# A graph network's gather: four tiles in every 320 loaded row by row from SyncE's queue

## The chip, the cores and the metric

One NeuronCore of a Trainium2 chip. The metric is the device time of one execution in microseconds, as the median of several runs. The kernel is written in Bass with the Tile framework, which puts the semaphores in and decides much of the order of instructions on each engine.

## The reference

Two layers of an equivariant graph network over the same graph: 6250 nodes with 160 features (64 scalars and 32 vectors of three components) and 200000 edges, sorted by destination. Each layer transforms the nodes, gathers the transformed row of every edge's source, multiplies it with weights that a small network makes from the edge's embedding and with the edge's attributes, sums over the edges of each destination, transforms the sums, and normalises. Of layer 0, cut to what matters here:

```python
x1s, x1v = ...                       # transformed nodes, 160 numbers a node
weight = silu(edge_length_embedded @ W_fc1) @ W_fc2
gs = x1s[edge_src]                   # the gather: one row of 640 bytes per edge
gv = x1v[edge_src]
mid0a = w0 * gs * e_s
...
agg = segment_sum(edge_feat, edge_dst, num_segments=n) / sqrt(16.0)
...
x = layernorm(x + layer0(x, ...))
x = layernorm(x + layer1(x, ...))
```

Layer 1 has the same form, with an embedding of 64 numbers per edge in place of 10 and 224 weights in place of 192. Everything is float32.

## The kernel before

**Tiles.** The edges are cut into 1563 tiles of 128 edges, one edge a partition (`NT`). Two tiles make a pair, two pairs a unit: 391 units. Each layer is one pass over the units in the function `windows(i, ...)`, i being 0 or 1. A prologue makes the first layer's table of transformed nodes, `table[0]`, in DRAM; pass 1 of the edges makes `table[1]` from its sums, and pass 2 gathers from that. (If the destinations don't fit the kernel's windows, another branch, `general`, computes everything; the inputs here don't take it.)

**The loop.** `windows` steps u from -4 to 391. In step u it issues
- `gather` for the pairs of unit u + 4: one indirect DMA per tile, issued by POOL (GpSimd), that fetches the 128 rows of `table[i]` named by the tile's sources into the tile `g` (L703). There are 8 buffers of `g`, one a pair;
- `weights` of unit u + 2 on PE (TensorE) and `hidden` of unit u + 3 on PE and ACT (ScalarE): the small network's two layers. `hidden` asks for the inputs `e`, a chunk of 8 tiles at a time, through SP's queue (SP is SyncE; `inputs`, L634 in pass 1, L642 in pass 2), into three tiles in turn (`inputs_of`). It asks for a chunk and the one after it;
- `places` and `products` of unit u + 2 on DVE (VectorE): the selection matrix from destinations and attributes (L734), and the products of gathered rows and weights, `mid` (L721);
- `aggregate` of unit u: matmuls on PE that sum the products by destination in PSUM; `turn` adds a finished group to the sums in SBUF (L778 loads the group's first destination into a register, L781 and L783 add);
- between these, `prepare` and `proceed` do the node work, one step at a time. `fetch` loads a block of nodes into the tile `nx` through SP (L486, L488, L545). In pass 1 `own_nodes` computes the self part of half of the blocks early, through a tile `ne` with one buffer, and stores it to DRAM (L471).

Sources (`src`) and attributes (`ea`) of 48 tiles are loaded at once through SP (`scalars`, L611 and L612), into two buffers each. The call stands where a tile of a new chunk is first needed:

```python
def of(t):
    if ("c", t // CH) not in made:
        scalars(t // CH)
```

**What sets the order.** On PE the order is the program's (`keep_in_program_order`, L138 and L143 are the helpers' lines, which all matmuls share). On the other engines and for the DMAs Tile's scheduler orders the instructions within what the data allow. SP's and ACT's DMAs go out in the order of their queues: an SP instruction that waits holds up all that stand behind it. Each of these DMAs uses one of eight completion semaphores in turn, and waits for the DMA that used it before.

Of the kernel before, what the change touches and what calls it, by code (L numbers as in the profile page):

```python
# [9 lines left out]
F32 = mybir.dt.float32  # L10
I32 = mybir.dt.int32
# [3 lines left out]
ET = mybir.EngineType  # L15

P = 128
N = 6250
E = 200000
S, V = 64, 32  # L20
D = S + 3 * V
NB = (N + P - 1) // P
NT = (E + P - 1) // P
# [3 lines left out]
CH = 48  # L27
EC = 8
BG = 4
ZERO = 8  # L30
ROWS = P * NB + P
EPS = 1e-5
C_S = math.sin(math.pi / 8.0)
# [53 lines left out]
def kernel(ctx: ExitStack, tc: tile.TileContext, a, out):  # L87
# [19 lines left out]
    nc = tc.nc  # L107
# [3 lines left out]
    work = prologue.enter_context(tc.tile_pool(name="first", bufs=2))  # L111
# [7 lines left out]
    table = [dram.tile([N, D], F32, name=f"table{i}") for i in range(2)]  # L119
# [30 lines left out]
    for bs in chunks:  # L150
        x = work.tile([P, BG, D], F32, name="xg", bufs=len(chunks))
# [67 lines left out]
    at = 0  # L219
# [244 lines left out]
    def own_nodes(b, work):  # L464

        n = rows_of(b)
        rows = slice(b * P, b * P + n)
        (fetch, self_part, self_mix), _ = second_nodes(b, work, False, "ne")

        def store():  # L470
            nc.scalar.dma_start(xown[rows, :], self_mix()[:n])  # L471
            owned.add(b)

        return [fetch, self_part, store]

    def second_nodes(b, work, clear, name="nx"):


        n = rows_of(b)
        rows = slice(b * P, b * P + n)  # L480
        st = {}

        def fetch():
            x = st["x"] = work.tile([P, D], F32, name=name, bufs=4 if name == "nx" else 1)
            if b in owned:
                nc.sync.dma_start(x[:n], xown[rows, :])  # L486
            else:
                nc.sync.dma_start(x[:n], a["x_main"][:, b, :] if b < NB - 1 else a["x_tail"])  # L488

        def self_part():  # L490
            st["xs"] = turned(st["x"][:n], work, "pn", 1)

        def self_mix():
            x = st["x"]
            q = mixed(st["xs"], n, wsc, "pn", 1)
            for k in range(2):
                nc.vector.scalar_tensor_tensor(x[:n], q[:, k, :], own[:n, b, k:k + 1], x[:n],
                                               op0=OP.mult, op1=OP.add)
            return x

        def summed():
            p = psum.tile([P, 512], F32, name="pn", bufs=1)
            q = p[:n, :2 * D].rearrange("p (w d) -> p w d", w=2)
            for c in range(4):
                l = sm[:96, c, rows]
                if c < 2:
                    matmul(q[:, :, 0:S + V], l, rm0[:, c], start=(c == 0), stop=False)
                else:
                    v = S + (c - 1) * V
                    matmul(q[:, :, 0:S], l, rm0[:, c, :, 0:S], start=False, stop=False)  # L510
                    matmul(q[:, :, v:v + V], l, rm0[:, c, :, S:], start=False, stop=False)
            matmul(q[:, :, S + V:D], sr[:64, rows], rr0, start=False, stop=True)
            y = st["x"][:n]
            for k in range(2):
                nc.vector.scalar_tensor_tensor(y, q[:, k, :], gets[:n, b, k:k + 1], y,
                                               op0=OP.mult, op1=OP.add)
            mv = work.tile([P, 8], F32, name="mv")
            normed(y, mv)

        def turn():  # L520
            st["xt"] = turned(st["x"][:n], work, "pn", 1)

        def mix():
            xt = st["xt"]
            p = psum.tile([P, 512], F32, name="pn", bufs=1)
            matmul(p[:n, 0:P], xt[:, 0, :n], who[0][:, :P], start=True, stop=True)
            matmul(p[:n, P:D], xt[:V, 1, :n], who[1][:, :V], start=True, stop=True)
            r = work.tile([P, D], F32, name="nr")
            nc.scalar.activation(r[:n], p[:n, 0:D], AF.Copy, scale=nv[:n, b, 0:1])
            nc.scalar.dma_start(table[1][rows, :], r[:n])  # L530
            nc.scalar.dma_start(xmid[rows, :], st["x"][:n])
            if clear:
                nc.vector.memset(sm[:, :, b * P:b * P + P], 0.0)
                nc.vector.memset(sr[:, b * P:b * P + P], 0.0)

        return [fetch] + [self_part, self_mix] * (b not in owned), [summed, turn, mix]
# [47 lines left out]
        return [fetch, self_part, self_mix], [summed]  # L584


    def windows(i, loads, work, inputs_of):
        nw = (192, 224)[i]


# [9 lines left out]
        made = {}  # L600
# [24 lines left out]
        def inputs(c):  # L625

            e0 = c * EC * P
            n = min(EC * P, E - e0)
            k, of_e = ((10, a["e10"]), (64, a["e64"]))[i]
            e = inputs_of[c % 3]  # L630

            for h in range(2):
                if i == 0 and n == EC * P:
                    nc.sync.dma_start(  # L634
                        e[h * 64:h * 64 + k].rearrange("p (u m) -> p u m", m=2 * P),
                        of_e[:, e0:e0 + n].rearrange("p (u h m) -> p u h m", h=2, m=2 * P)[:, :, h])
                    continue
                for u in range(0, n, 4 * P):
                    r = u + h * 2 * P
                    m = min(2 * P, n - r)  # L640
                    if m > 0:
                        nc.sync.dma_start(e[h * 64:h * 64 + k, u // 2:u // 2 + m],  # L642
                                          of_e[:, e0 + r:e0 + r + m])
            made["e", c] = e
# [34 lines left out]
        def weights(ps):  # L679
# [5 lines left out]
            for p, j in [(p, j) for p in ps for j in range(2)] if i == 0 else \  # L685
                    [(p, j) for j in range(2) for p in ps]:
                t = 2 * p + j
                if t < NT:
# [5 lines left out]
                        l, r = h[k, j * P:j * P + n], fc2[1][k]  # L694
                    matmul(made["w", p][:n, j, :nw], l, r, start=True, stop=True)

        def gather(p):
            g = work.tile([P, 2, D], F32, name="g", bufs=8)
            for j in range(2):
                t = 2 * p + j  # L700
                if t < NT:
                    n = edges_of(t)
                    nc.gpsimd.indirect_dma_start(  # L703
                        out=g[:n, j, :], out_offset=None, in_=table[i][:, :],
                        in_offset=bass.IndirectOffsetOnAxis(ap=of(t)[0], axis=0))
            made["g", p] = g
# [117 lines left out]
        for u in range(-4, units + 1):  # L824
# [7 lines left out]
                weights(pairs_of(u + 2))  # L832
            if 0 <= u + 3 < units:
                hidden(u + 3)
            if 0 <= u + 2 < units:
                for p in pairs_of(u + 2):
                    places(p)
                    products(p)
# [131 lines left out]
    with tc.If(ok > 0) as cmp:  # L970
        with tc.tile_pool(name="loads", bufs=2) as loads, \
                tc.tile_pool(name="edges", bufs=2) as work:

            inputs_of = [loads.tile([P, EC * P // 2], F32, name=f"e{k}", bufs=1) for k in range(3)]
            for e in inputs_of:
                nc.vector.memset(e, 0.0)
            for i in range(2):
                windows(i, loads, work, inputs_of)
    with cmp.Else():
        pinned[0] = False  # L980
        owned.clear()
# [54 lines left out]
```

## Time and profile before

| | |
|---|---|
| median of 3 runs | 4095.0 us (4084.81 to 4096.76) |
| the profiled execution | 4098.12 us, its span 4096.3 us |
| mean granted clock of TensorE | 0.900 |
| busy in the span | PE 3522.1 us (86%), DVE 3095.1 us (76%), POOL 3026.7 us (74%), ACT 1176.1 us (29%) |
| POOL's gathers, L703 | 3126, the first starts at 65.8 us, the last at 4056.9 us |
| pause of POOL between the passes | 34.6 us, for the last blocks of nodes |
| moved by DMA | 364.05 MB, 89 GB/s on average |

Busy time is an average over the span; an engine that is busy for less than all of it may still be the one that all others wait for, if each of its instructions is followed by a fixed pause. SP computes nothing: its instructions are DMA issues, waits and register steps, and the profile does not count them as busy. They are seen in the timeline and by line, where a duration is the time that the issue takes on SP's queue, not the transfer's.

The profile's lines name the kernel's lines; "out<-in" are tiles. For a group, the numbers are the busy time in us, the mean in ns, and the engine's idle time just before its instructions with what ended most of it.

### The profile page before, as it was taken

The page shows a single profiled execution, that of the slowest core. Times are in us where ns is not written, and L with a number is a line of the kernel's source. Part 1 is how long each engine was busy: PE and PEld are TensorE (multiplying, and loading weights), DVE is VectorE, ACT ScalarE, POOL GpSimd, SP SyncE. Part 2 cuts the span into 40 slices and gives each one's busy share as a digit, 9 for nine tenths or more (in the row PEclk, how much of TensorE's full clock was granted, in tenths as well). Part 3 has the DMA queues.
Part 4 walks back from the last instruction along what each step waited for, and adds up shares of the span by engine and source line. Part 5 has one row for each costly group of instructions (what it writes and reads, how often), then busy time and mean ns, then how long its engine had stood idle before and what let it go on. Part 6 is the DMA issues. An engine that isn't in the chain of part 4 may idle for free. (4 is left out here: it accounts for less than half of the span.)

```text
span 4096.3 us, 108196 instructions
## 1 busy us (share of the span) xinstructions
PE 3522.1 (86%) x37363; PEld 2419.1 (59%) x37363; DVE 3095.1 (76%) x13202; ACT 1176.1 (29%) x4013; POOL 3026.7 (74%) x3232
## 2 busy tenths in 40 slices
PE   7788988889899999999978888888788888888887
PEld 5565666666666666666655555555555555555555
DVE  6676666667777777777757777777778888888887
ACT  2122221222222333333311111122223333444454
POOL 4777777777777777777757777777777777777774
PEclk8899898889899999999978888889989999998998
DMA  4233322222222232333323333333333333333332
GB/s 128 78 84 87 81 75 77 78 76 79 77 79 79 79 82 79 82 84 80 87 71 94 96 95 97 98 96 96 100 97 97 103 100 96 106 100 98 101 103 59
DMA packets 298517, 364.05 MB, mean 89 GB/s; under 512 B 86323, under 2 KB 246204, under 8 KB 297964
## 3 DMA queue, kind: packets, MB, share of 16 engines
q0 software_dynamic: 151056, 257.36, 23.8%
q1 hardware_dynamic: 121740, 85.59, 7.4%
q10 hardware_dynamic: 25168, 14.11, 1.1%
q8 instruction: 300, 4.92, 0.5%
q14 instruction: 253, 2.07, 0.2%
HBM read 338.73 MB, written 18.03 MB: 87 GB/s over the span
## 5 line engine op out<-in xcount | busy, mean ns | idle before, releaser
L703 POOL DMA_INDIRECT g<-table,src x3126 | 3004.9, 961 | 1026.8 <-issue 736.9
L721 DVE TENSOR_TENSOR mid<-g,pw 128x128 f32<-128x128 f32 (+2 forms) x7820 | 1852.8, 299 | 653.0 <-DMA g<-table,src 416.1
L138 PE MATMUL pw<-fc,h 100*128 100x192 f32 (+1 forms) x6252 | 1225.5, 383 | 193.4 <-DVE mid L721 186.4
L138 PE MATMUL pg<-mid,sel 128*32 128x160 f32 (+1 forms) x25008 | 1155.1, 305 | 0.0
L138 PEld LDWEIGHTS pw<-fc,h 100*128 100x128 f32 (+1 forms) x6252 | 895.9, 203 | 369.9 <-issue 315.0
L138 PEld LDWEIGHTS pg<-mid,sel 128*32 128x32 f32 x25008 | 755.3, 116 | 387.7 <-issue 320.7
L734 DVE SCALAR_TENSOR_TENSOR sel<-iota,off,ea 128x128 f32<-128x128 f32 x3126 | 940.5, 341 | 39.4 <-PE pg L138 35.0
L138 PE MATMUL pair<-e,fc 64*100 64x256 f32 (+1 forms) x2348 | 606.2, 454 | 120.2 <-DVE sr L783 113.4
L665 ACT ACTIVATE h<-pair 100x256 f32<-100x256 f32 x782 | 260.7, 381 | 954.6 <-PE pair L138 941.0
L138 PEld LDWEIGHTS pair<-e,fc 64*100 64x100 f32 (+1 forms) x2348 | 239.5, 183 | 351.2 <-issue 193.1
L676 ACT ACTIVATE h<-pair 128x256 f32<-128x256 f32 x392 | 150.5, 384 | 960.5 <-PE pair L138 795.6
L143 PE MATMUL pair<-ident,r 128*96 128x128 f32 (+1 forms) x852 | 225.7, 291 | 27.6 <-ACT h L665 21.7
L138 PE MATMUL pn<-rm,sm 96*128 96x128 f32 (+4 forms) x980 | 192.1, 356 | 51.2 <-DVE sm L781 49.6
L759 ACT ACTIVATE r<-pg 128x96 f32<-128x96 f32 (+1 forms) x568 | 149.5, 263 | 297.8 <-PE pg L138 228.5
L781 DVE TENSOR_TENSOR sm<-pair,sm 96x128 f32 (+1 forms) x568 | 161.9, 285 | 92.1 <-PE pair L143 19.1
L143 PEld LDWEIGHTS pair<-ident,r 128*96 128x96 f32 (+1 forms) x852 | 107.8, 127 | 206.0 <-issue 105.3
L765 ACT ACTIVATE rest<-pg 32x32 f32<-32x32 f32 x1136 | 209.5, 184 | 12.5
L138 PEld LDWEIGHTS pn<-rm,sm 96*128 96x128 f32 (+3 forms) x980 | 176.3, 235 | 59.9 <-DVE sm L781 53.3
L138 PE MATMUL pn<-rr,sr 64*128 64x128 f32 (+2 forms) x196 | 66.1, 426 | 93.4 <-DVE sr L783 89.0
L458 ACT ACT_TABLE_LOAD x97 | 124.5, 1283 | 7.1 <-DVE mv L457 5.4
L138 PEld LDWEIGHTS pair<-fold,rest 128*128 128x128 f32 x568 | 104.0, 226 | 1.1 <-ACT rest L765 1.1
L783 DVE TENSOR_TENSOR sr<-pair,sr 64x32 f32 (+1 forms) x568 | 99.7, 176 | 0.8 <-DVE sm L781 0.6
(137 smaller groups left out, 1313.0 us busy)
## 6 DMA issues: line engine op xcount, KB each, us to landing
g<-table,src POOLq DMA_INDIRECT x3126
e<-in_e SPq DMA_DIRECT2D x781, 64.0 KB
e<-in_e SPq DMA_DIRECT2D x390, 20.0 KB
ea<-in_ea_main SPq DMA_DIRECT2D x63, 96.0 KB
xg<-in_x_main SPq DMA_DIRECT2D x12, 320.0 KB
table<-rg SPq DMA_DIRECT2D x12, 320.0 KB
xmid<-nx ACTq DMA_DIRECT2D x48, 80.0 KB
table<-nr ACTq DMA_DIRECT2D x48, 80.0 KB
```

Source lines behind the costliest of these rows:

```text
L138: r = nc.tensor.matmul(*args, **kw)
L143: r = nc.tensor.transpose(*args)
L458: nc.scalar.activation(mv[:n, 1:2], mv[:n, 1:2], AF.Sqrt, bias=eps[:n])
L665: nc.scalar.activation(h[:100, 2 * P * j:2 * P * j + m], pair[j][:100, :m], AF.Silu)
L676: nc.scalar.activation(h[:kk, c0:c1], p[:kk, c0:c1], AF.Silu, scale=0.125)
L703: nc.gpsimd.indirect_dma_start(out=g[:n, j, :], out_offset=None, in_=table[i][:, :], in_offset=bass.IndirectOffsetOnAxis(ap=of(t)[0], axis=0))
L721: nc.vector.tensor_tensor(parts(mid[:n, :m], V * place, V * step, k), parts(g[:n, :m], c, V, k), parts(q[:n, :m], w, w_step, k), OP.mult)
L734: made["last"] = nc.vector.scalar_tensor_tensor(s[:n, j], iota[:n, None, :].to_broadcast([n, 4, W]), w, e[:, :, None].to_broadcast([n, 4, ...
L759: nc.scalar.activation(r[:, :w], pg[:, :w], AF.Copy)
L765: nc.scalar.activation(rest[g % 3][k, k], pg[k, P:P + V], AF.Copy)
L781: nc.vector.tensor_tensor(sm[:h, :, at], pt[:h, :P].rearrange("p (c w) -> p c w", c=4), sm[:h, :, at], OP.add)
L783: made["last"] = nc.vector.tensor_tensor(sr[:k, at], pt[:k, P:P + W], sr[:k, at], OP.add)
```

## The change

Units 80, 160, 240 and 320 of each pass (`ROW_UNITS`) are no longer gathered by POOL. Their four tiles have a buffer of their own, `gs`, of which there is one. `rows_of_unit(u)` fills it through SP's queue in the steps between one such unit and the next (77 steps, for unit 80 it is 76): SP reads the sources of two partitions, eight numbers, into registers (`TensorLoad`), and for each of them issues a DMA of one row of 640 bytes, `table[i]` at the register's row. That is 64 reads and 512 DMAs for a unit, spread evenly, 0.83 reads and 6.6 DMAs in a step; the last stands in step x - 5 for unit x, whose products stand in step x - 2. In the built program each DMA has one register instruction ahead of it, which turns the row's number into an address. The rows' instructions on SP keep the program's order. The sources for this are loaded once, ahead of the first pass, into `row_src`.

To make room, `e` has two tiles in place of three, and `ne` is gone: `own_nodes` uses the tile `no` of pass 2 (four buffers, 192 wide). And `scalars` is called for the next chunk in the step in which the tiles gathered reach the middle of a chunk.

```diff
+ROW_UNITS = range(80, (NT + 3) // 4 - 1, 80)
...
-        (fetch, self_part, self_mix), _ = second_nodes(b, work, False, "ne")
+        (fetch, self_part, self_mix), _ = second_nodes(b, work, False, "no")
...
-            x = st["x"] = work.tile([P, D], F32, name=name, bufs=4 if name == "nx" else 1)
+            x = st["x"] = work.tile([P, D if name == "nx" else 192], F32, name=name, bufs=4)[:, :D]
...
-            e = inputs_of[c % 3]
+            e = inputs_of[c % 2]
...
+        def rows_of_unit(u):
+
+            k = next((k for k, x in enumerate(ROW_UNITS) if x - 4 >= u), None)
+            begin = 0 if not k else ROW_UNITS[k - 1] - 1
+            if k is None or u < begin:
+                return
+            x = ROW_UNITS[k]
+            if u == begin:
+                made["rows", x] = work.tile([P, 4, D], F32, name="gs", bufs=1)
+            g, steps, m = made["rows", x], x - 4 - begin, P // 2
+            for q in range((u - begin) * m // steps, min((u - begin + 1) * m // steps, m)):
+                loads_, v = nc.values_load_multi_w_load_instructions(
+                    row_src[q:q + 1, k].rearrange("q h t -> q (h t)"), engines=[ET.SP], min_val=0,
+                    max_val=N - 1,
+                    skip_runtime_bounds_check_because="an edge's source is a node")
+                for r in loads_:
+                    in_order(r)
+                for h in range(2):
+                    for j in range(4):
+                        in_order(nc.sync.dma_start(g[2 * q + h:2 * q + h + 1, j, :],
+                                                   table[i][bass.ds(v[4 * h + j], 1), :]))
+
         def gather(p):
+            if p // 2 in ROW_UNITS:
+                made["g", p] = made["rows", p // 2][:, 2 * (p % 2):2 * (p % 2) + 2, :]
+                return
...
+            c, at = divmod(4 * (u + 4), CH)
+            if at == CH // 2 and (c + 1) * CH < NT:
+                scalars(c + 1)
+            rows_of_unit(u)
...
-            inputs_of = [loads.tile([P, EC * P // 2], F32, name=f"e{k}", bufs=1) for k in range(3)]
+            inputs_of = [loads.tile([P, EC * P // 2], F32, name=f"e{k}", bufs=1) for k in range(2)]
...
+            row_src = loads.tile([P // 2, len(ROW_UNITS), 2, 4], I32, name="row_src", bufs=1)
+            for k, u in enumerate(ROW_UNITS):
+                nc.sync.dma_start(row_src[:, k], a["src_main"][:, 4 * u:4 * u + 4, 0].rearrange(
+                    "(q h) t -> q h t", h=2))
```

More of the change, by code (lines that the diff above doesn't have):

```diff
@@ L584, in last_nodes, with windows @@
         return [fetch, self_part, self_mix], [summed]
-    def windows(i, loads, work, inputs_of):
+    def windows(i, loads, work, inputs_of, row_src):
         nw = (192, 224)[i]
@@ L695, in weights, with in_order @@
                     matmul(made["w", p][:n, j, :nw], l, r, start=True, stop=True)
+        def in_order(r):
+            tc.keep_in_program_order(r)
+        def rows_of_unit(u):
[18 more added lines that the diff above has]
+                                                   table[i][bass.ds(v[4 * h + j], 1), :]))
         def gather(p):
+            if p // 2 in ROW_UNITS:
+                made["g", p] = made["rows", p // 2][:, 2 * (p % 2):2 * (p % 2) + 2, :]
+                return
             g = work.tile([P, 2, D], F32, name="g", bufs=8)
@@ L972 @@
                 tc.tile_pool(name="edges", bufs=2) as work:
-            inputs_of = [loads.tile([P, EC * P // 2], F32, name=f"e{k}", bufs=1) for k in range(3)]
+            inputs_of = [loads.tile([P, EC * P // 2], F32, name=f"e{k}", bufs=1) for k in range(2)]
             for e in inputs_of:
                 nc.vector.memset(e, 0.0)
+            row_src = loads.tile([P // 2, len(ROW_UNITS), 2, 4], I32, name="row_src", bufs=1)
+            for k, u in enumerate(ROW_UNITS):
+                nc.sync.dma_start(row_src[:, k], a["src_main"][:, 4 * u:4 * u + 4, 0].rearrange(
+                    "(q h) t -> q h t", h=2))
             for i in range(2):
-                windows(i, loads, work, inputs_of)
+                windows(i, loads, work, inputs_of, row_src)
     with cmp.Else():
```

## Prediction

> **What bounds the kernel now.** I read the page first, then POOL's timeline in the middle of a pass, then DVE's waits at L721 by stretches, then SP's issues one line at a time.
>
> From the page, the two groups that meet:
>
> ```profile
> L703 POOL DMA_INDIRECT g<-table,src x3126 | 3004.9, 961 | 1026.8 <-issue 736.9
> L721 DVE TENSOR_TENSOR mid<-g,pw 128x128 f32<-128x128 f32 (+2 forms) x7820 | 1852.8, 299 | 653.0 <-DMA g<-table,src 416.1
> ```
>
> POOL's 3004.9 us of gathers and 1026.8 us of idle time fill nearly the whole span, and DVE's largest wait at L721 is for gathered rows. POOL's timeline tells whether that idle time is slack:
>
> ```profile
> 2705.49 0.95 POOL L703 DMA_INDIRECT g<-table,src  x1 [0.30 <-issue]
> 2706.74 0.95 POOL L703 DMA_INDIRECT g<-table,src  x1 [0.30 <-issue]
> 2708.00 0.95 POOL L703 DMA_INDIRECT g<-table,src  x1 [0.30 <-issue]
> 2709.25 0.95 POOL L703 DMA_INDIRECT g<-table,src  x1 [0.30 <-issue]
> ```
>
> It is not: one gather follows the other every 1.25 us (0.95 us of work, 0.30 us before the next). 3126 x 1.25 is 3908 us of 4096. So POOL's gathers are the bound, at 5.0 us per unit of four tiles. The exceptions are late in each pass. This is what DVE waited for at L721, first in 2560 to 3060 us, then in 1707 to 2020 us:
>
> ```profile
>   DMA g<-table,src: 75.3, 105
>   PE pw L138: 14.2, 23
> ```
> ```profile
>   PE pw L138: 9.9, 18
> ```
>
> In the second stretch no product waited for a gather, and by the windows POOL ran 244 gathers in 313 us, 1.28 us each, with PE busy for 289.6 us of the 313. There PE and DVE set the pace by a little. 3640 to 4058 us is alike (no wait for a gather).
>
> SP's present issues, and the two register steps that the change adds to SP (seen here on DVE's queue):
>
> ```profile
> L488 SPq DMA_DIRECT2D ne<-in_x_tail x1: 247/247/247, 494.4 to 494.4; - x1
> L634 SPq DMA_DIRECT2D e<-in_e x390: 282/284/1258, 65.9 to 2022.1; - x195
> L424 SPq DMA_DIRECT2D rm<-in_lin_wv x12: 310/420/527, 34.5 to 43.9; - x12
> L642 SPq DMA_DIRECT2D e<-in_e x784: 282/551/1587, 2022.9 to 4036.4; - x196
> L778 DVEq TENSOR_LOAD <-base x568: 297/304/601, 97.8 to 4083.7; - x190
> L778 DVEq FUSED_REGOPS  x568: 190/190/206, 98.2 to 4084.1; - x190
> L781 DVEq FUSED_REGOPS  x568: 69/69/75, 98.5 to 4084.3; - x190
> ```
>
> The three numbers are the shortest, median and longest time in ns. An issue holds SP for 0.25 to 0.55 us, whatever it moves. FUSED_REGOPS takes 190 ns right behind the load whose register it reads, 69 ns elsewhere.
>
> **Removed from POOL.** Units 80, 160, 240 and 320 of each pass: 2 x 4 x 4 = 32 gathers at 1.25 us, 40 us. What of it arrives at the end depends on where it falls. At the page's pace unit 80 is near 470 us and unit 320 near 1690 us of pass 1; in pass 2 they are near 2490 and 3700 us. Units 80, 160 and 240 lie where DVE still waits for gathers, so their 5 us each become an earlier start of all that follows. Unit 320 opens the stretch that PE and DVE pace; a POOL that is ahead there only fills its buffers. I count 15 us for pass 1 and 17 us for pass 2 (its late stretch is less tight: PE is busy for 425 of 498 us): 32 us. What is late next is PE's and DVE's own work.
>
> **Added to SP.** Each unit is 64 reads of eight sources and 512 loads of one 640-byte row, each with a register step that makes its address. No row of the trace is a load of one row from a register's address. The nearest are 106 rows in 0.247 us, 10 rows (each in two pieces) in 0.284 us, 32 rows in 0.420 us. I take 0.28 us, the load of the fewest rows; the ends are 0.25 and 0.42 us. Between two SP instructions lie about 0.045 us (L424 in the timeline starts at 35.07, lasts 0.43, and the next starts at 35.54). A row is then 0.07 + 0.28 + 2 x 0.045 = 0.44 us. A read of sources adds 0.30 for the load, 0.12 for the first register step's longer wait, 0.05 for the gap: 0.47 us. Eight rows with their read: 8 x 0.44 + 0.47 = 4.0 us; a unit's 64: 255 us.
>
> Per 80 units SP also issues, in pass 1, 80 loads of e at 0.34 us with their gap (27 us), in pass 2 160 at 0.61 us (98 us), and chunks and node rows for some 10 us. So SP needs 292 us of pass 1's and 363 us of pass 2's 80 units, for which POOL needs 79 x 5.0 = 397 us. With rows of 0.25 and 0.42 us pass 2 would need 348 and 435 us. At 0.28 SP keeps up, at 91% in pass 2, and the whole of its work lies beside POOL's. That is the cover: without it every us that SP is over per 80 units counts four times in pass 2.
>
> [...]
>
> **Waits that the change adds.** SP and ACT take eight completion semaphores in turn, and each DMA waits for the one eight before it. L424's loads went out 0.46 us apart without a wait, so a small load lands within 8 x 0.46 = 3.7 us; a row's turn comes round in 4.0 us. No wait. Behind a waiting SP stand the loads of e, for which PE's L138 pair waits, and so everything. With two buffers in place of three, a chunk of e is asked for when PE has done with the one before last: three units, 15 us, ahead of its use, in place of five. PE's queue shows no wait for e now but one of 5.9 us at the start. I cost it at nothing: the cover is these 15 us, and SP may be some 10 us behind before it shows. The products of a row unit wait for 512 rows, the last asked for three units (15 us) ahead: nothing.
>
> **Small edits.** Chunks of src and ea half a chunk ahead: no POOL or DVE wait for them stands in the waits today, so nothing. The tile no in place of ne (four buffers for one) takes away PE's 62 us of waits for ne in the first 500 us, where POOL is the bound: nothing. The four loads of row_src go ahead of the first loads of e, some 2 us, while POOL fills its sixteen tiles of buffers (20 us): nothing.
>
> **Sum.** 4098.1 us for the profiled execution less 32 us is 4066 us; it lay 3 us over the median of 4095.0, so 4063 us for the median.
>
> **Rivals.** (1) SP becomes the bound of pass 2: slower. A row load is like the 32-row one, 0.42 us. Then a unit is 64 x (8 x 0.58 + 0.47) = 327 us, with 98 + 10 us beside it 435 us per 80 units against the present 403: +32 us, four times, less 10 us that SP may lag: +118 us; with pass 1's gain of 15 us, 4198 us. For it: the 0.42 and 0.55 us rows, and an address from a register that no load of the trace has. Against it: the loads of 10 and of 106 rows, both under 0.29 us in the median. It decides from 0.35 us per row load (397 us less 108 and 64 x 0.47, over 512, less 0.16); at 0.36 us gain and loss cancel.
>
> (2) PE and DVE take POOL's place earlier: same. PE is busy for 376 of 408 us in 1299 to 1707 us already. If from unit 160 on nothing of the 5 us arrives, only units 80 count: 10 us, 4085 us. Against it: 75 us of waits for gathers in 500 us of pass 2.
>
> (3) All of it arrives: if a POOL that is ahead helps late in the passes as well, 40 us, 4055 us.
>
> **How the numbers follow.** The measurement tells 0.3% (12 us) from no change. Forecast and rival (3), 4050 to 4080 us: 0.62. Rival (2), and SP a little over its time: 0.12. Rival (1), 4107 us and up, according to the row's cost: 0.26. The low end of the range is 40 us off the fastest of the three runs (4084.8), 4045; upward it takes in rival (1) up to a row load of 0.40 us (4158 us by the same sum) and 7 us for the spread of the runs above: 4165 us. The likeliest case's own range is 4048 to 4082 us.
>
> **What would show it.** Right: 3094 gathers still 1.25 us apart; SP's row loads near 0.28 us and register steps near 0.07; no wait of DVE for gs; no wait of PE for e; DVE's wait for gathers below 416 us. Wrong: row loads over 0.35 us, SP without idle time in pass 2, PE waiting for e, POOL's gathers held up by their buffers between 2100 and 3700 us.

## The result and the profile after

The changed kernel takes 4138.5 us in the median of seven runs (4122.6 to 4149.6), the kernel before 4091.2 us in seven runs (4084.8 to 4096.8). The ratio is 1.0112, with a 95% interval of 1.0087 to 1.0136: slower by 47 us. I had forecast 4063 us, faster. The sign is wrong. The time lies inside the range by luck: the range went up to 4165 us only for dear row loads, and the row loads were not dear (below).

The profiled execution took 4138.5 us, with a span of 4136.7 us and a mean granted clock of 0.888 (before: a span of 4096.3 us and 0.900). Line numbers of the changed kernel: gathers L732 (were L703), products L750 (L721), loads of e L635 and L643 (L634 and L642), the reads of sources L712 and the rows L720 (new).

From the page, the groups that answer to those of before (busy us, mean ns of one, then idle us before them and what ended most of it):

```profile
L732 POOL DMA_INDIRECT g<-table,src x3094 | 2982.9, 964 | 1089.4 <-issue 729.6
L750 DVE TENSOR_TENSOR mid<-g,pw 128x128 f32<-128x128 f32 (+2 forms) x7740 | 1822.1, 298 | 423.8 <-DMA g<-table,src 205.5
L139 PE MATMUL pair<-e,fc 64*100 64x256 f32 (+1 forms) x2348 | 611.9, 458 | 142.6 <-DMA e<-in_e 78.8
L144 PE MATMUL pn<-ident,nx 128*128 128x128 f32 (+1 forms) x244 | 62.8, 346 | 208.8 <-DMA nx<-xmid 124.6
```

The 32 gathers are gone, and VectorE's wait for gathered rows has halved, from 416.1 to 205.5 us. That is what the change was to bring. What is new stands in the last two rows: TensorE now waits for data that SP fetches. The chunks of e cost it 78.8 us (5.9 before), and the node rows nx, which its transposes need, cost 124.6 us and more. TensorE's waits for DMAs (us in total, times, longest us):

```profile
PE pn L144 <- DMA nx<-xmid: 124.6, 23, 10.6
PE pair L139 <- DMA e<-in_e: 78.8, 33, 6.1
PE pn L144 <- DMA nx<-in_x_main: 66.9, 14, 8.6
PE pn L144 <- DMA no<-in_x_main: 29.8, 14, 3.7
```

Before, TensorE waited for no nx; for ne, the tile whose place no has taken, it waited 29.2 us. POOL is still at 1.25 us from gather to gather where it runs, but it is now held up by its buffers; before, the same wait was 110.3 us, 361 times, 0.5 us at most:

```profile
POOL g L732 <- DVE mid L750: 170.8, 329, 9.4
```

SP's queue shows why the data came late, and the reason differs between the passes. SP's waits at the rows over the whole span:

```profile
SPq L720 <- DMA xmid<-nx: 143.2, 23, 17.4
SPq L720 <- DMA xown<-no: 50.1, 15, 10.7
SPq L720 <- DMA table<-nr: 47.2, 20, 8.8
SPq L720 <- DMA out<-nx: 30.8, 10, 12.0
```

All four are stores of node rows, and ACT issues them, not SP. SP and ACT take the same eight completion semaphores in turn. A row whose turn fell on the semaphore of a store waited until that store had landed, and a store that ACT had not yet issued, since its data was still being made, landed late. In the trace the wait is in all 68 cases one of the row's own DMA, for the very semaphore that it then uses itself. This is such a place, from the timeline of SP:

```profile
2436.67 2.39 SPq L643 DMA_DIRECT2D e<-in_e  x4
2440.29 15.42 SPq L720 DMA_DIRECT2D gs<-table  x8
2456.02 0.36 SPq L612 DMA_DIRECT2D src<-in_src_main  x1
```

and of ACT:

```profile
2448.39 0.29 ACT L459 ACTIVATE mv<-mv,eps 128x1 f32<-128x1 f32 x1 [0.17 <-DVE mv L458]
2450.48 0.37 ACTq L583 DMA_DIRECT2D out<-nx  x1
```

Eight rows took 15.42 us: SP stood still for 12.0 us after the first, until ACT had issued the store of out at 2450.48 and it had landed; the second row went out at 2452.68. Whatever SP had in its queue behind them (chunks, e, node rows) waited as well.

In pass 2 such stalls are few: from 2203 to 3753 us (units 20 to 320) SP stood still for 72 of 1550 us. There SP is simply full. Summed over its instructions with the gaps behind them, the 1953 rows took 811 us, the loads of e 388 us, 244 reads of sources 234 us. SP's own work is 394 us per 80 units, against POOL's 397. In SP's timeline no stall is to be seen, only one thing after the other, and the fetch of node rows (L546) last:

```profile
2773.77 2.68 SPq L720 DMA_DIRECT2D gs<-table  x7
2776.55 2.39 SPq L643 DMA_DIRECT2D e<-in_e  x4
2780.14 7.63 SPq L720 DMA_DIRECT2D gs<-table  x16
2789.06 2.39 SPq L643 DMA_DIRECT2D e<-in_e  x4
2792.67 3.13 SPq L720 DMA_DIRECT2D gs<-table  x8
2795.86 0.35 SPq L546 DMA_DIRECT2D nx<-xmid  x1
```

TensorE had come to that transpose at 2787.4 us:

```profile
2786.62 0.75 PE L139 MATMUL pg<-mid,sel 128*32 128x160 f32 x16
2797.96 0.69 PE L144 MATMUL pn<-ident,nx 128*128 128x128 f32 x2 [10.59 <-DMA nx<-xmid]
2798.58 1.30 PE L139 MATMUL pg<-mid,sel 128*32 128x160 f32 x16
```

The wait costs more than its 10.59 us. Sixteen matmuls that took 0.75 us before it take 1.30 us after it: the granted clock is 1.00 from 2783 to 2787 us and 0.50 from 2798 to 2802 us. So it is after most long waits: over the 90 waits of TensorE that are longer than 2 us the granted clock is 0.95 on average in the 4 us before, and 0.56 in the 3 us after.

The kernel asks for node rows one step, about 5 us, before the transpose that needs them, and TensorE's order is fixed: nothing behind the transpose goes ahead. So a fetch that is issued more than a few us late becomes idle time of TensorE at once, and after 8 buffers of g that of POOL.

When it was lost can be read off the starts of VectorE's first sel of each unit, after minus before. In pass 1 the changed kernel is 9.5 us ahead at unit 180, where 10 us were forecast for two row units. Single starts scatter: from unit 165 to 195 it is 1 to 12 us ahead, and at unit 35, before the first row unit, it was 15 us ahead for a while. From unit 200 to 320 it loses 43 us net: units 200 to 320 take 658 us where they took 615. There TensorE has no time to spare (before, it was busy for 634 of the 688 us from 1050 to 1738), and now waits 43.3 us for nx and 13.1 us for e between 1043 and 1738 us. Of the 43 us, 28 are more idle time of TensorE in these units (78.8 us in place of 50.3). The other 15 are more busy time (579.6 us in place of 564.9) for the same number of matmuls (5955 and 5954 records), at a granted clock of 0.89 in place of 0.92. It enters pass 2 31 us behind. Between units 20 and 320 of pass 2, where TensorE waits for nx 124.6 us and for e 50.3 us, it falls back by another 16 us instead of gaining; most of those waits go into slack that it had there (its wait for products fell from 152 to 67 us, VectorE's for gathers from 186 to 81 us).

One thing the profile leaves open. SP also stands still at the loads of e until TensorE has freed one of the two tiles, in pass 1 for 30.7 us from 173 to 1043 us and 48.1 us from there to 1738 us (L635 <- PE pair). How much of the lateness behind it is due to that, and so to the third tile that was given up, no run shows by itself; without rows it costs nothing (small_edits, below).

### The profile page after: what moved, and what is told of

Its sections match the earlier page's. It is cut to its first block, busy times and chain, and to the rows that moved or that the text cites. A ratio compares the mean times of both kernels' runs of the same rounds, so it can differ in the third digit from the quotient of the medians.

```text
span 4136.7 us, 121053 instructions
## 1 busy us (share of the span) xinstructions
PE 3491.4 (84%) x37363; PEld 2397.5 (58%) x37363; DVE 3083.2 (75%) x13201; ACT 1177.6 (28%) x4013; POOL 3004.6 (73%) x3200
## 5 line engine op out<-in xcount | busy, mean ns | idle before, releaser
L732 POOL DMA_INDIRECT g<-table,src x3094 | 2982.9, 964 | 1089.4 <-issue 729.6
L750 DVE TENSOR_TENSOR mid<-g,pw 128x128 f32<-128x128 f32 (+2 forms) x7740 | 1822.1, 298 | 423.8 <-DMA g<-table,src 205.5
L139 PE MATMUL pw<-fc,h 100*128 100x192 f32 (+1 forms) x6252 | 1195.4, 385 | 107.2 <-DVE mid L750 87.5
L139 PEld LDWEIGHTS pw<-fc,h 100*128 100x128 f32 (+1 forms) x6252 | 886.2, 205 | 257.4 <-issue 191.4
L139 PE MATMUL pair<-e,fc 64*100 64x256 f32 (+1 forms) x2348 | 611.9, 458 | 142.6 <-DMA e<-in_e 78.8
L144 PE MATMUL pn<-ident,nx 128*128 128x128 f32 (+1 forms) x244 | 62.8, 346 | 208.8 <-DMA nx<-xmid 124.6
L139 PE MATMUL pn<-rm,sm 96*128 96x128 f32 (+4 forms) x980 | 172.5, 330 | 23.3 <-DVE sm L810 21.7
L139 PEld LDWEIGHTS pn<-rm,sm 96*128 96x128 f32 (+3 forms) x980 | 157.2, 213 | 31.6 <-DVE sm L810 25.4
L144 PEld LDWEIGHTS pn<-ident,nx 128*128 128x128 f32 (+1 forms) x244 | 21.3, 133 | 237.5 <-DMA nx<-xmid 133.2
L441 ACT ACTIVATE xt<-pn 128x128 f32<-128x128 f32 x147 | 40.6, 276 | 268.5 <-PE pn L144 268.1
```

The lines of the kernel that those rows point to most:

```text
L139: r = nc.tensor.matmul(*args, **kw)
L144: r = nc.tensor.transpose(*args)
L441: nc.scalar.activation(xt[:, 0, :n], p[:, 0:n], AF.Copy)
L732: nc.gpsimd.indirect_dma_start(out=g[:n, j, :], out_offset=None, in_=table[i][:, :], in_offset=bass.IndirectOffsetOnAxis(ap=of(t)[0], axis=0))
L750: nc.vector.tensor_tensor(parts(mid[:n, :m], V * place, V * step, k), parts(g[:n, :m], c, V, k), parts(q[:n, :m], w, w_step, k), OP.mult)
```

## The experiments

The chips that were to be had for the experiments granted TensorE a clock of 0.74 to 0.77, and the kernel before took 5925 to 6038 us on them, so every time stands as a ratio to the kernel before in the same batch, and what depends on POOL's pace could not be repeated. The sign of that regime is POOL's wait for buffers in the version without rows (small_edits):

```profile
POOL g L732 <- DVE mid L750: 1761.9, 470, 10.1
```

There TensorE and VectorE set the pace throughout, about 7.2 us per unit (units 20 to 320 of small_edits). What keeps SP's queue late can be tested well in it, the worth of a gather badly.

**The changed kernel there (after_again).**

> The changed kernel, unaltered, on the chip that granted TensorE's clock 0.76 to the earlier experiments (the kernel before takes about 5925 us there). It is the mark for all of them. From two row units per pass at 1.0192, I expect twice that, 1.038 (6150 us). If the node rows behind the rows are the loss (theory), it is well above the version with node rows two steps ahead (1.0318) and the version with node rows on ACT's queue (1.0338), by the 190 us that TensorE waits for nx in the version whose rows nobody uses: 1.05 and more. If it is at 1.03 to 1.04 too (rival), moving the node fetches alone repairs nothing: the wait only goes on to e.

Ratio 1.0454 (1.0421 to 1.0487): 264 us in the medians, more than the 1.038 that I expected from the half version. It lies between the ratios that I had set for the theory (1.05 and more) and for the rival (1.03 to 1.04), so it does not decide between them. TensorE waits 112.1 us for nx from xmid, 80.2 us for nx from the input, 61.5 us for e: the same picture as in the first profile. That its price is larger I put down to TensorE, which has no slack here; no run shows it.

**Small edits alone (small_edits).**

```
-ROW_UNITS = range(80, (NT + 3) // 4 - 1, 80)
+ROW_UNITS = range(0)
```

> The changed kernel without any row unit: POOL gathers all 3126 tiles again, SP issues no rows; two tiles of e, the tile no in place of ne and the earlier chunks stay. Theory A (SP's rows hold up the node rows nx and the chunks of e in SP's queue, and PE, whose order is fixed, waits for them): the small edits cost little by themselves, 4085 to 4100 us, and PE's waits for nx and e fall to some 20 us. Rival B (the two tiles of e cost the time): 4110 us and over, with PE waiting for e for 50 us and more.

Ratio 0.9999 (0.9975 to 1.0024). Two tiles of e, the tile no and the earlier chunks cost nothing there; TensorE's only wait for e is one of 5.7 us at the start, and for nx there is none.

**The gathers taken away without the rows (bulk_rows, and once more as bulk_rows_again).**

```
+            for j in range(4):
+                if u == begin + 1 + 2 * j:
+                    in_order(nc.sync.dma_start(g[:, j, :], table[i][j * P:(j + 1) * P, :]))
```

> The changed kernel with the 2048 + 256 x 2 row instructions of a unit's 512 rows replaced by four DMAs of 128 consecutive rows each; it leaves out which rows are gathered (the row units multiply the first 512 rows of the table). POOL issues 3094 gathers as in the changed kernel, SP is as free as before. Theory A: the whole gain of POOL arrives, 4055 to 4070 us. Rival C (taking 32 gathers from POOL brings nothing, because PE and DVE are the bound): 4085 to 4095 us.

> The row units' 512 rows each are replaced by four DMAs of 128 consecutive rows (other rows than the sources, so other values), with the 32 gathers still gone and the two e tiles, the tile no and the earlier chunks kept. It tells what the missing gathers are worth where POOL is the bound. My prediction's sum: 32 us less, about 4060 us where the kernel before takes about 4092. Rival: PE and DVE set the pace so often that only 10 us come through, 4080 us. If the two e tiles cost by themselves, it is 4092 or over.

Ratios 0.995 (0.9924 to 0.9977) and 0.9954 (0.9938 to 0.9971): 27 to 30 us less. In microseconds that is near my 32, but not for my reason, since POOL is not the bound there; what 32 gathers are worth at POOL's pace is not measured by it. It does show that on these chips everything lost by the changed kernel is lost by how the rows are fetched.

**The rows without their use (rows_unused).** POOL gathers every unit, SP loads the rows all the same.

> SP loads all rows as in the changed kernel, but nobody uses them: POOL gathers every unit as before (3126 gathers). It tells the price of the rows alone. Theory (rows hold up what stands behind them on SP; the gathers' gain is real): slower than the changed kernel by 20 to 40 us, 4160 to 4180 us, PE's waits for nx about as in the changed kernel. Rival (the gathers' removal gains nothing, or the products' own wait for the row tile is the loss): about the same as the changed kernel (4130 to 4145) or near the kernel before (4092).

Ratio 1.0525 (1.0495 to 1.0555), above the changed kernel's 1.0454 in another batch: the loss is not in the products that use the row tile.

**Stores off ACT's queue (pool_stores).**

```
-            nc.scalar.dma_start(xown[rows, :], self_mix()[:n])
+            nc.gpsimd.dma_start(xown[rows, :], self_mix()[:n])
```

and the same for table, xmid and out.

> The stores of node rows (xown, table, xmid, out) are issued on POOL's queue, by software descriptors, instead of ACT's, so that no row on SP has to wait for a semaphore of a store that ACT issues late. POOL gets some 280 more DMAs of about 1 us; where TensorE and VectorE set the pace (clock 0.76) POOL has 1700 us of waiting for buffers to spare, where POOL sets it they cost up to 280 us. Theory 1 (semaphores shared with ACT's stores): SP's waits at the rows for stores vanish, with them most of TensorE's waits for nx and e, and the ratio falls from the changed kernel's to 1.01 or less. Theory 2 (SP's occupation): the waits for nx and e stay at half or more and the ratio above 1.02.

Ratio 1.0205 (1.0173 to 1.0237): over half of the changed kernel's loss in the same batch is gone. SP's waits at the rows for stores are gone; of its waits for DMAs at L720 only those for earlier rows are left, short ones. TensorE's waits for nx and e fall from 254 to 8 us:

```profile
SPq L720 <- DMA gs<-table: 84.0, 171, 1.4
```
```profile
PE pair L139 <- DMA e<-in_e: 6.6, 2, 5.9
PE pn L144 <- DMA nx<-xmid: 1.8, 2, 1.0
```

So the shared semaphores are what makes nx and e late there, as theory 1 had it; but 1.0205 is not the 1.01 that it expected, and theory 2 expected the waits to stay. Neither is right as it stood: the waits go, and a rest of 2% stays.

**Rows from fixed addresses (rows_static).** Neither reads of sources nor register steps are left.

```
-                                                   table[i][bass.ds(v[4 * h + j], 1), :]))
+                                                   table[i][8 * q + 4 * h + j:8 * q + 4 * h + j + 1, :]))
```

> The rows are loaded from fixed addresses (512 consecutive rows of the table, so other values): no reads of sources by SP, no register steps, but the same 4096 one-row DMAs in the same places with the same semaphores. SP's time per eight rows falls from 4.15 us to about 8 x 0.27 = 2.2 us. Theory 1 (SP's semaphore waits for stores that ACT has yet to issue are the loss): SP still waits at the rows for xmid, xown, table and out, TensorE for nx and e, and at least three quarters of the changed kernel's loss stay. Theory 2 (SP's occupation, the sum of its own instructions, is the loss): at least half of the loss is gone, and the waits for nx and e with it.

Ratio 1.0111 (1.0063 to 1.0158): three quarters of the loss gone, and TensorE waits 7.2 us for nx and no time for e. SP still waits at the rows for stores of ACT (table 60.6 us, xmid 25.5, xown 19.7), but it has the time to make up for that: a stall did harm only where SP was too busy to catch up. Occupation and semaphores worked together, and either remedy freed TensorE.

**Reads of sources alone (reads_only).** The 512 reads stay, the rows come as in the bulk version.

> SP reads the sources of the row units, eight at a time (512 reads of 0.85 us), and loads no row for them; four DMAs of 128 consecutive rows per unit fill the tile (other values). It prices the reads alone against the bulk version (0.995) and the fixed-address version (1.011, no reads). If SP's occupation by itself were the loss, 435 us of reads would cost about as the 4096 fixed-address DMAs' 1040 us do, in proportion: ratio about 1.00 to 1.005. If a read on SP disturbs other engines' registers or issue by itself, it is above 1.015.

Ratio 0.9967 (0.9945 to 0.9990): the reads by themselves cost nothing that can be told from the bulk version.

**Half the rows (half_units): every 160th unit.**

> The changed kernel with units 160 and 320 alone loaded row by row, 64 reads and 512 rows spread over some 157 steps: SP has half of the row work in each step, POOL has 16 gathers less than the kernel before in place of 32. Theory A: SP is 75% occupied in pass 2, PE's waits for nx fall to a half or less, 4075 to 4100 us. Rival D (each row unit costs a fixed time where its products wait for the rows): half of the loss, about 4115 us.

Ratio 1.0192 (1.0154 to 1.0231), TensorE waiting 0.9 us for nx and 5.7 us for e. So there is a cost that is no wait for either. Whether it goes with the number of rows is not shown: pool_stores, with all the rows and nearly no such waits, stands at 1.0205, hardly above.

**Node rows two steps earlier (node_ahead).**

```
+                if first_:
+                    first_[:0] = [lambda: None] * 2
```

> The changed kernel with two empty steps between the fetch of a block of nodes and its first use on PE: its load is asked for three steps (15 us) ahead in place of one (5 us). Theory A: PE's waits for nx (208 us in the changed kernel with those for weight loads apart: 67 us in pass 1, 125 us in pass 2) nearly vanish, and pass 1 gets its 40 us back; pass 2 stays at SP's pace; in all 4075 to 4105 us. Rival B (two tiles of e): as the changed kernel, 4125 to 4145 us.

Ratio 1.0318 (1.0277 to 1.0359). The waits for nx vanish (2.5 us left), and the waits for e rise to 101.5 us: what stood behind the rows was served one item after the other, and the lateness moved to the next one.

**Node rows from ACT's queue (act_nodes), and e as well (act_both).**

```
-                nc.sync.dma_start(x[:n], xmid[rows, :])
+                nc.scalar.dma_start(x[:n], xmid[rows, :])
```

> The changed kernel with one thing moved: the fetches of node rows (nx, no) are issued on ACT's queue instead of SP's, so that they no longer stand behind the rows; the rows and the loads of e stay on SP. Theory (the loss is PE, whose order is fixed, waiting for node rows that stand in SP's queue behind rows held up to 17 us): PE's waits at L144 for nx<-xmid (124.6 us) and nx<-in_x_main (66.9 us) fall below 20 us in all; pass 2 loses its 10 us and more, and the time is 4090 to 4110 us where the kernel before takes about 4090; what is left is PE waiting for e (78.8 us), which may grow. Rival A (the loss is the rows' own traffic and SP's saturation, wherever the nodes are fetched): PE's waits move to e in full and the time stays at 4130 to 4145. Rival B (ACT's queue is itself too busy): the stores and h are late, slower than 4145.

> As act_nodes, and the loads of e go on ACT's queue too: SP issues rows, their reads, chunks of src and ea, and nothing that PE waits for. Theory: neither nx nor e is late behind a row any more; PE's waits for nx and e fall below 30 us together and the 32 us that the gathers save come through at least in part: 4060 to 4085 us. What can still stand in the way is ACT's queue, where an issue of 0.3 to 0.6 us delays h: 472 loads of e in pass 1 and 2 times as many half loads in pass 2 are about 1170 issues, 500 us spread over 4100, on an engine that has idle time. Rival A (rows disturb the gathers or DMA in general): POOL's gathers come at more than 1.25 us pitch or g is late, and the time stays above 4120. Rival B (ACT then sets the pace): ACT shows waits behind e's issue and the time is above 4100.

1.0338 (1.0308 to 1.0368) and 1.0709 (1.0680 to 1.0738). The first says the same as node_ahead: no wait for nx is left, and e is at 175.5 us. The second is a miss for all that I had expected. TensorE waits for neither, but the rows now take turns with the loads of e on ACT's queue, and SP is held up by those, and then by the chunks of sources, which POOL needs:

```profile
SPq L720 <- DMA e<-in_e: 790.7, 211, 16.0
SPq L612 <- DMA g<-table,src: 315.0, 15, 74.6
PE pw L139 <- DVE mid L750: 173.0, 35, 32.5
```

It is the shared semaphores again, with more DMAs on the other queue: moving a load to ACT's queue did not part it from the rows.

**Three tiles of e and earlier node rows (e3_ahead),** paid for with 7 buffers of g and 3 of no.

> The changed kernel with room given to both things that TensorE waits for: node rows fetched two empty steps earlier, and three tiles of e in place of two (paid for with 7 instead of 8 buffers of g and 3 instead of 4 of no). Rows and their reads stay on SP as they are. Theory (the loss is what stands behind the rows on SP, nx and e, and nothing else): TensorE's waits for nx and e fall below 20 us each, and the time is at or below the version without row units (ratio 1.00, at best 0.995 as with the bulk rows). Rival (the rows disturb something else, or SP lacks the time): the ratio stays above 1.02.

Ratio 1.0288 (1.0259 to 1.0316), hardly better than node_ahead in another batch, against the expectation. With 121.7 us the waits for e are longer still. With the third tile SP waits less at the loads of e for TensorE to free one (843 us, where after_again has 1053), but the load of e stays at the same place of SP's queue, behind the same rows, and at those SP still waits 372 us for stores (398 in after_again).

**The best that seemed possible (half_ahead): half the rows, node rows two steps earlier.**

> Only units 160 and 320 are row units (half the rows per step), and node rows are fetched two empty steps ahead: the most of the change that SP seems to have time for. At a granted clock of 0.90 and POOL's pace: 16 gathers less are 20 us, SP needs some 210 to 260 of each 400 us, TensorE waits for neither nx nor e: 4072 to 4085 us where the kernel before takes 4091, the one version that could beat both. At a clock of 0.75: as the half version without the earlier node rows, ratio 1.015 to 1.02, since that version already waited for neither.

Ratio 1.0162 (1.0137 to 1.0187). No version with row loads beat the kernel before on these chips.

**An attempt to get POOL's pace back (light_before, light_after, light_bulk, light_static).**

```
-            for c, (at, step, k) in enumerate(sums):
+            for c, (at, step, k) in enumerate(sums if first else sums[:1]):
```

> The kernel before with TensorE's work cut: of the four matmuls that sum a tile's products, only the first tile of each group issues all four, the others one (so most sums are left out). The chips of the experiments grant TensorE a clock of about 0.75, and it sets the pace there; with a third less of its work POOL's gathers should be the bound again, as in the profiled execution of the kernel before. I expect 4100 to 4500 us, POOL's waits for buffers (1760 us in the version without rows at full work) under 500 us. If TensorE or VectorE still set the pace, POOL's wait stays above 1000 us and the other three tell nothing new.

> The changed kernel with TensorE's work cut in the same way. My prediction's steps (POOL bound, SP keeps up, nothing waits behind the rows) give 30 to 40 us less than the cut kernel before. Theory (SP is held up at rows by semaphores and is nearly full in pass 2, nx and e behind it come late for TensorE): TensorE still waits over 150 us for nx and e, some of which its new slack covers, and it is 20 to 80 us slower than the cut kernel before; the faster pace makes SP fuller still (5.0 us per unit leaves 400 us per 80 units for 390 of SP's own work in pass 2).

> The cut kernel with four DMAs of 128 consecutive rows in place of a row unit's 512 (other values), small edits as in the changed kernel. The gathers' worth where POOL is the bound: 30 to 40 us less than the cut kernel before, if my prediction's first step holds. If the two tiles of e or another small edit cost something under POOL's pace, the gain is below 20 us and TensorE waits for e.

> The cut kernel with the rows loaded from fixed addresses (other values): the same 4096 one-row DMAs, without reads and register steps, SP's time per 80 units 265 us less 125 or so. If SP's occupation is the loss, it comes to the bulk version's time within 15 us, and TensorE's waits for nx and e are gone. If the shared semaphores are, at least half of the difference between the changed and the bulk version stays.

It failed in its aim: the cut kernel before took 5539 us, far over the 4100 to 4500, and POOL still waited 1377 us for its buffers. Fewer matmuls, 22015 in place of 37363, did not bring TensorE's pace down in proportion (the time fell to 0.9363). Still it repeats the order of the others in a second setting. Against the cut kernel before, the changed one is at 5863 / 5539 = 1.058, the bulk version at 5533 / 5539 = 0.999, fixed addresses at 5585 / 5539 = 1.008. The last is 52 us over the bulk version, more than the 15 that I had allowed if SP's occupation were the whole loss. But it keeps 16% of the 330 us between the changed kernel and the bulk version, not the half that the semaphores alone would have kept.

**The rest that stays open.** On these chips there are stretches of some us in which SP and TensorE are slow at the same time, TensorE with waits that are put down to issue. It has such waits without any rows too (689 us in small_edits); whether the lower clock of these chips comes of them, or they of it, no run shows. SP's timeline in the half version, beside that of TensorE:

```profile
576.15 4.27 SPq L720 DMA_DIRECT2D gs<-table  x5
```
```profile
576.89 0.48 PE L139 MATMUL pw<-fc,h 100*128 100x192 f32 x2 [0.70 <-issue]
578.31 0.48 PE L139 MATMUL pw<-fc,h 100*128 100x192 f32 x2 [0.94 <-issue]
579.74 0.80 PE L139 MATMUL pw<-fc,h 100*128 100x192 f32 x2 [0.94 <-issue]
```

Five rows took 4.27 us, where seven with nothing else between them took 2.68 in the first profile, and TensorE's pairs of matmuls started 1.42 and 1.43 us apart beside them. A row's two register steps, 0.048 and 0.038 us at most in the first profile, took up to 0.756 and 1.386 us in after_again. TensorE's waits of this kind are 689 us in small_edits, 777 in half_units, 785 in pool_stores, and 0.2 us in the profile of after. The rest of 1 to 2% in half_units, pool_stores and rows_static may be such stretches, made more or longer by SP's row instructions (12288 of them in the changed kernel, 6144 in the half version, 4096 with fixed addresses); no run tells that apart from the row DMAs' own load. Nor does one tell it apart from the granted clock, which lay at 0.749 to 0.750 in the four executions of pool_stores and at 0.753 to 0.759 in the seven of the kernel before beside them. The stretches have no counterpart in the first profile.

So the two remedies, other semaphores and less work on SP, are shown to free TensorE on these chips. For the chip of the first profile the same two causes are read from its trace, from the 68 waits and from SP's 394 us per 80 units; there neither was taken away.

## Why the prediction was wrong

**The gathers: right.** They stayed 1.25 us apart, and the 10 us of the first two row units of pass 1 were there at unit 180 (9.5 us), within the scatter. In pass 2 the first row unit shows more plainly: the changed kernel is 33.6 us behind at unit 80, 27.5 at unit 85 and 28.7 at unit 100. So POOL was the bound there, before SP's lateness took the gain back. Two readings were not exact: in the late stretches, where I wrote that no product waited for a gather, the same views have 5.8 us of such waits (1707 to 2020 us) and 3.4 us (3640 to 4058 us). And 79 x 5.0 us is 395, not 397. Neither changes the argument.

**The row on SP: right, a little dear.** A row load took 0.228 us in the median, under my 0.28. From the views of one line:

```profile
L712 SPq TENSOR_LOAD <-row_src x512: 709/804/998, 85.7 to 3738.8; - x171
L720 SPq FUSED_REGOPS  x4096: 37/37/48, 86.5 to 3742.7; - x196
L720 SPq MOVE gs<-table x4096: 29/29/38, 86.6 to 3742.8; - x196
L720 SPq DMA_DIRECT2D gs<-table x4096: 224/228/307, 86.7 to 3742.8; - x196
```

With its two register steps and three gaps of some 0.04 us, a row goes out every 0.41 us; I had 0.44.

**The read of sources: mis-sized.** I took SP's TENSOR_LOAD from VectorE's (0.30 us) and made the read 0.47 us. It took 0.80 us in the median, and 0.96 us on the average of pass 2 with its gap (234 us for 244). A row of SP's own, for one register, was in the profile of before, and I passed it over; with it the read would have come to 0.73 us:

```profile
L969 SPq TENSOR_LOAD <-flag x1: 564/564/564, 61.9 to 61.9; - x1
```

The errors do not cancel: per 80 units of pass 2 the rows took 216 us where I had 225, the reads 62 where I had 30, and the loads of e 103 where I had 98. SP's own work came to 394 us, not 363. "SP keeps up, at 91%" was 99% of POOL's pace, with nothing left for a stall.

**"Waits that the change adds. No wait": the step that failed.** I asked how long a DMA takes to land (3.7 us) and compared it with the turn of the eight semaphores (4.0 us). In the first profile that holds for rows behind rows: no row waited 0.15 us or more for another (in after_again 126 did, 1.4 us at most). But ACT's stores take their turns too, and a store held its semaphore from the place in the order where it stands, not from when it was issued. Until ACT gets to it, all of TensorE's, VectorE's and ACT's work on that block of nodes lies in between. So SP, whose work was meant to run ahead of the other engines, was tied to their progress 68 times, for 271 us at the rows in all, 17.4 us at the longest. Moving the stores off ACT's queue took these waits away on the experiments' chips, and TensorE's with them (254 to 8 us).

**"Behind a waiting SP stand the loads of e ... the cover is these 15 us": incomplete and too hopeful.** I named e and left out the node rows, which are on the same queue with a cover of one step, 5 us. They cost TensorE 124.6 + 66.9 us for nx and 29.8 us for no, and the clock, which was at 0.56 on average after such waits, had no term in my sum. And the cover of e is used up by SP's lateness, not by one stall: 78.8 us.

**"Small edits: nothing".** On the experiments' chips that held (0.9999); at POOL's pace it was not measured alone. The 62 us that I gave for ne added TensorE's 29.2 us and its weight loads' 33.1 us, which wait at the same time; what the tile no took away came back as the 29.8 us for no.

**The rivals.** The first, SP as the bound of pass 2, had the right engine and sign and the wrong condition. It was to decide at 0.35 us per row load, and the load took 0.228. Two things that it did not price did it: the read, and the stalls. It also priced SP's work as a throughput, from the point where it exceeds POOL's; the loss began before that, in pass 1, where SP's own work is about three quarters of the time (1184 of 1565 us from 173 to 1738 us), because what counts is how late a single fetch is. The second rival's TensorE bound explains where it hurt: in units 200 to 320 of pass 1 TensorE had no slack to lose. What I listed as signs of a wrong forecast, SP without idle time in pass 2, TensorE waiting for e and POOL held up by buffers (29.2 us from 2100 to 3700 us, before 8.2), are what the profile shows; the fourth, row loads over 0.35 us, did not come.

## What to carry to other kernels

Before work is put on a queue that looks idle, list every transfer behind it in program order with its lead over the instruction that needs it; the shortest lead is the cover, not that of the largest transfer. Then look for who shares completion semaphores with the queue: a DMA of another engine that waits for computed data turned a queue that prefetches into one that ran in step with the computation (68 rows, 271 us). And if lateness is repaired at one waiter alone, expect it at the next: here it moved from nx (2.5 us left in node_ahead) to e (101.5 us) until SP's work or the semaphores themselves were relieved.

## What the runs showed of the hardware

A TENSOR_LOAD of eight registers took SP 0.80 us, where VectorE's load of one, the group's first destination, took 0.30; the one load of the flag at L969 of the kernel before took 0.56 on both. An address from a register made the issue of a one-row DMA on SP no dearer: 0.228 us in the median in the changed kernel, 0.225 on the experiments' chips, where the same load from a fixed address took 0.250.

After waits of TensorE of more than 2 us the granted clock was 0.56 on average in the next 3 us, and 0.95 in the 4 us ahead of them (90 waits of the changed kernel's first profile); in the profile of before it was 0.62 and 0.97 (67 waits).

With 22015 matmuls instead of 37363, on a chip that granted 0.77, the time fell by 6% only (0.9363, 0.9322 to 0.9404). And in the half version's profile, at 0.76, five rows took SP 4.27 us from 576.15 us on, while TensorE started pairs of matmuls 1.42 and 1.43 us apart; TensorE's waits put down to issue are 777 us there, and 0.2 us in the first profile, at 0.89.
